# Where a chunk's first two passes over its adjacency stand in the VectorE queue of a four-layer graph network

## The chip, the cores and the metric

The kernel runs on one core of one Trainium2 chip. A core has a matrix engine (TensorE, in the profile PE, with its weight loads as PEld), a vector engine (VectorE, DVE), a scalar engine (ScalarE, ACT), a general engine (GpSimd, POOL) and a synchronisation engine (SyncE, SP), which here issues most DMA transfers. The engines run at the same time, each working through its own queue of instructions, and wait for one another through semaphores. The metric is the device time of one execution in microseconds (us), the median of several runs. The span is the same thing as one profiled execution shows it, from its first to its last instruction.

## The reference

Four layers work on a batch of 128 graphs of 64 nodes with 256 features each, and on one 64x64 adjacency matrix per graph. Each layer ends with a residual sum and a layer norm.

```python
def reference(x, adj, nodemask, ...):        # x (128, 64, 256), adj (128, 64, 64)
    # layer 0: five groups of nodes out of the first 25, two normalised graph convolutions each
    x = _layernorm(x + _L0_gnn_ref(x, adj, W1, b1, W2, b2, fusion_w))
    # layer 1: one normalised graph convolution
    x = _layernorm(x + _L1_gnn_ref(x, adj, W, b))
    # layer 2: polynomial of degree 3 in the row-normalised adjacency
    x = _layernorm(x + _L2_gnn_ref(x, adj, W, conv_w, conv_b))
    # layer 3: five steps of message passing with a GRU cell
    x = _layernorm(x + _L3_gnn_ref(x, adj, nodemask, weight, w_ih, w_hh, b_ih, b_hh))
    return x

# layer 0, for each group of nodes (25, 9, 7, 6 and 6 of them)
A = adj_g + eye;  dinv = sum(A, -1) ** -0.5
norm_adj = dinv[:, :, None] * A * dinv[:, None, :]
h   = relu(norm_adj @ (x_g @ W1[g]) + b1[g])
out = relu(norm_adj @ (h @ W2[g]) + b2[g])

# layers 1 and 2 on the whole 64x64 adjacency
deg_inv_sqrt = (adj + eye).sum(-1) ** -0.5
adj_norm = adj / (adj.sum(2, keepdims=True) + 1e-9)
```

What matters below: layer 0 makes a scaled and transposed adjacency for every group, and layers 1 to 3 make others (row sums, a normalised matrix, a matrix of zeros and ones) from the whole 64x64 adjacency of each graph.

## The kernel before

Layer 0 is cut into 16 *units*: numbers 0 to 8 belong to the four small groups of nodes, numbers 9 to 15 to the group of 25 (`g0` is 9). Layers 1 to 3 are cut into 16 *chunks* of 8 graphs. The order of TensorE's instructions is that of the program text. The other engines' instructions are put in order at compile time: an instruction may be placed ahead of others that stand before it in the text, as soon as what it needs is, by the compiler's reckoning, at hand.

A unit of layer 0 is prepared like this. It reads its slice `a` of the adjacency, takes the power -0.5 of the degrees on GpSimd, spreads the result into block-diagonal form (`A0`), has TensorE transpose it, and scales the transposes on the way out of PSUM:

```python
powers, evictions, relus = [], [], []

def prep(i):                                             # cut
    u = UNITS[i]
    scale, last = [], evictions[-1] if evictions else None
    for ts, nb, r, k in u.same:
        with tc.issue_after(last.ins) if last else nullcontext():
            nc.vector.tensor_add(ae[...], a[...], eye0[...])             # A + eye
        nc.vector.tensor_reduce(deg[:r], av, AX.X, ALU.add)
        dinv = inv_sqrt(deg[:r], w, r, "d0")             # d0z, d0s on DVE, d0r on POOL, d0o on DVE
        nc.vector.tensor_mul(av, av, dinv[...])
        nc.vector.tensor_mul(A0[...], ae[...], block0[...])              # block diagonal
        nc.tensor.transpose(p[:r, t, :r], A0[:r, t, :r], ident[:r, :r])  # one per tile
        scale.append((AT[...], p[...], dinv[...]))
    for v in scale:
        with tc.high_priority():
            evictions.append(nc.vector.tensor_mul(*v))   # the scaling of the unit's transposes
```

`tc.issue_after(ins)` makes each instruction of its block stand behind `ins` in the queue of `ins`'s engine. It adds an order at compile time and no semaphore.

A chunk of layers 1 and 2 goes through the generator `mid`; only its first piece matters here:

```python
def load_adj(c):
    a64 = keep.tile([128, NP, N], F32, name="a64", bufs=2)
    nc.sync.dma_start(a64, av[c])
    adjs[c] = a64

def mid(c):
    a64 = adjs.pop(c)
    Ab = keep.tile([128, NP, 128], F32, name="Ab", bufs=1)
    nc.vector.tensor_mul(Ab..., a64..., pair...)                    # two graphs as one 128x128 block
    A01 = keep.tile([128, NP, 128], F32, name="A01", bufs=4)
    nc.vector.tensor_scalar(A01, Ab, 0.0, None, op0=ALU.not_equal)
    rsum = small.tile([128, NP], F32, name="rsum")
    nc.vector.tensor_reduce(rsum, a64, AX.X, ALU.add)
    # rdeg, rinv, reciprocal, dinv1 = inv_sqrt(rdeg, ..., "d1"), rsum + 1e-9: small, from rsum
    nc.vector.tensor_mul(dg, ident..., rsum...)
    nc.scalar.activation(poly, dg, AF.Identity, scale=cw[:, 2:3])
    nc.vector.tensor_mul(An, Ab, rinv...)
    yield
    # ... TensorE transposes Ab (pT1), DVE makes AT1 from it
    yield
    # ... six further pieces: polynomial, gathers, products, norms
```

Layer 0's loop over the units calls pieces of the first two chunks in between (`early_stage` takes `mid(0)` and then `mid(1)` on by one `yield`):

```python
early = both(mid(0), mid(1))
places = [(1, 1), (1, 2), (2, 1), (2, 2), (2, 2), (3, 1), (3, 2), (3, 2)]
places += [(4, 0), (4, 0), (4, 1), (4, 2), (4, 2), (5, 1), (5, 2), (5, 2)]     # (i - g0, place)

for i in range(-2, NU + 1):                              # cut
    stage(load0, i + 3)
    stage(add, i - 1)
    stage(aggregate, i + 1)
    early_stage(i, 0)
    stage(support, i)
    stage(finish, i - 1, g0)
    early_stage(i, 1)
    stage(prep, i + 2)
    stage(hidden, i + 1)
    early_stage(i, 2)
    # store_others(i - 1), others(i), load_others(i + 2): layer norm of the nodes outside every group
    if i == g0:
        for c in (0, 1):
            load_adj(c)
    # ...
```

So in the program's text the first piece of `mid(0)` comes in turn i = 10, after `prep(11)` and before `prep(12)`, and that of `mid(1)` in turn i = 13, after `prep(14)`. For the chunks 2 to 15 the two loads and `mid` are called from layer 3's loop, when layer 0 has long been written down.

Of the kernel before, what the change touches and what calls it, by code (L numbers as in the profile page):

```python
# [11 lines left out]
ALU = mybir.AluOpType  # L12
AX = mybir.AxisListType
PSUM = bass.MemoryType.PSUM

B, N, D, HID, L = 128, 64, 256, 512, 5
# [11 lines left out]
NP = CB // 2  # L28
# [40 lines left out]
def gnn_stack(  # L69
# [26 lines left out]
    nc = tc.nc  # L96
# [17 lines left out]
    powers, evictions, relus = [], [], []  # L114
# [63 lines left out]
    def psum(name):  # L178
        return pt.tile([128, 512], F32, tag="pt", name=name)

    def psum0(name):

        taken[0] += 1
        if taken[0] % 8 < 5:
            return pg.tile([128, 512], F32, tag="pg", name=name)
        return psum(name)
# [33 lines left out]
    def mid(c):  # L220

        a64 = adjs.pop(c)


        Ab = keep.tile([128, NP, 128], F32, name="Ab", bufs=1)
        nc.vector.tensor_mul(
            Ab.rearrange("p q (b m) -> p q b m", b=2),
            a64[:, :, None, :].to_broadcast([128, NP, 2, N]),
            pair[:, None, :, :].to_broadcast([128, NP, 2, N]),
        )  # L230
        A01 = keep.tile([128, NP, 128], F32, name="A01", bufs=4)
        nc.vector.tensor_scalar(A01, Ab, 0.0, None, op0=ALU.not_equal)
        rsum = small.tile([128, NP], F32, name="rsum")
        nc.vector.tensor_reduce(rsum, a64, AX.X, ALU.add)
        rdeg = small.tile([128, NP], F32, name="rdeg")
        nc.vector.tensor_scalar(rdeg, rsum, 1.0, None, op0=ALU.add)
        rinv = small.tile([128, NP], F32, name="rinv")
# [17 lines left out]
        p = psum("pT1").rearrange("p (q n) -> p q n", q=NP)  # L255
# [10 lines left out]
        p = psum("pp").rearrange("p (q n) -> p q n", q=NP)  # L266
# [7 lines left out]
        p = psum("pp").rearrange("p (q n) -> p q n", q=NP)  # L274
# [6 lines left out]
        for u in range(NP // 2):  # L281
            p = psum("pd").rearrange("p (q d) -> p q d", q=2)
            for h in range(2):
                q = 2 * u + h
# [4 lines left out]
            for h in range(2):  # L289
                q = 2 * u + h  # L290
# [11 lines left out]
        for u in range(NP // 2):  # L302
            p = psum("pd").rearrange("p (q d) -> p q d", q=2)
            for h in range(2):
                q = 2 * u + h
# [5 lines left out]
            for h in range(2):  # L311
                q = 2 * u + h
# [13 lines left out]
    def const_later(src, shape, name):  # L326
        return const(src, shape, name, nc.gpsimd)
# [5 lines left out]
    with ExitStack() as c0:  # L333
# [198 lines left out]
        p = psum0("pw")  # L532
# [22 lines left out]
        def products(l, q):  # L555
# [7 lines left out]
            return p  # L563

        early = both(mid(0), mid(1))

        places = [(1, 1), (1, 2), (2, 1), (2, 2), (2, 2), (3, 1), (3, 2), (3, 2)]
# [11 lines left out]
        for i in range(-2, NU + 1):  # L579
# [54 lines left out]
            elif i == 1:  # L634
                with tc.issue_after(powers[-1].ins):
                    pair = const_later(c_pair, [128, 2, N], "pair")
# [284 lines left out]
    for s in range(NCH * L):  # L921
        u, t = s // (2 * L) * 2, s % (2 * L)
        if t == 0:
            for _ in filler:
                pass
            if u + 2 < NCH:
                for c in (u + 2, u + 3):
                    load_adj(c)
                    load_x(c)
                filler = both(mid(u + 2), mid(u + 3))  # L930
# [116 lines left out]
```

## Time and profile before

| quantity | value |
|---|---|
| device time, median of 3 runs | 2215.43 us (2214.81 to 2216.5) |
| span of the profiled execution | 2214.5 us |
| mean clock granted to TensorE | 0.994 |
| instructions | 30166 |
| HBM traffic over the span | 22 GB/s |
| DVE, two stretches of 20 us: 80 to 100 and 100 to 120 us | 5.20 and 0.75 us busy |
| ACT, the same two | 6.29 and 0.00 us busy |
| PE, the same two | 20.00 and 6.35 us busy |

Layer 0 takes roughly the first 320 us, and layers 1 to 3 the rest. An engine's busy time is the time in which an instruction of its is recorded as running. "Granted clock" is the share of full speed at which TensorE was let run. In the timelines a row gives the start in us, the time from the first to the last instruction of the row, the engine, the line of the program, the operation, the output and the inputs with their shapes, how many instructions the row merges, and in brackets how long the engine had been idle and what ended that wait. A wait is told as "engine, what it waited to do, whom it waited for".

### The profile page before, as it was taken

How to read it: one execution, taken by the hardware profiler on the slowest of the kernel's cores; microseconds unless marked ns; L12 is line 12 of the kernel's file. 1: busy time of each engine (PE TensorE's matmuls, PEld its weight loads, DVE VectorE, ACT ScalarE, POOL GpSimd, SP SyncE). 2: the span in 40 equal slices, each digit the busy share in tenths (PEclk: the TensorE clock that was granted, in tenths of full speed). 3: DMA queues.
4: the chain of work that ended last, by engine and by line, in shares of the span. 5: the costliest groups of instructions: out<-in, count | busy, mean ns of one | idle time of the engine just before them, and what ended most of it. 6: DMA issues, size and time to landing. Idle time of an engine off the chain costs nothing.

```text
span 2214.5 us, 30166 instructions
## 1 busy us (share of the span) xinstructions
PE 2180.2 (98%) x11542; PEld 1911.4 (86%) x11542; DVE 1372.5 (62%) x3088; ACT 1003.1 (45%) x1853; POOL 571.0 (26%) x621
## 2 busy tenths in 40 slices
PE   9979999999999999999999999999999999999997
PEld 6657888888889889888889898888898898888886
DVE  3344666665766666666766676657666666566546
ACT  3233334445545454445454454455454544455453
POOL 3211122222222223223222222222222232232221
PEclk9989999999999999999999999999999999999999
DMA  5531210000100000000100010001000000000000
GB/s 166 178 109 55 58 46 4 1 3 1 41 1 4 1 20 22 3 1 7 35 1 3 1 41 1 3 1 41 1 1 1 20 10 1 1 10 11 1 1 20
DMA packets 54172, 51.12 MB, mean 23 GB/s; under 512 B 20878, under 2 KB 49036, under 8 KB 54028
## 3 DMA queue, kind: packets, MB, share of 16 engines
q1 hardware_dynamic: 49664, 43.96, 6.5%
q0 software_dynamic: 1936, 4.83, 0.8%
q8 instruction: 91, 1.49, 0.3%
q10 hardware_dynamic: 2428, 0.41, 0.1%
q14 instruction: 53, 0.43, 0.1%
HBM read 32.40 MB, written 16.78 MB: 22 GB/s over the span
## 4 chain that ended last, share of the span: by engine, by line
PE 94%; SPq 2%; DVE 1%; issue 1%; DMA 1%; ACT 0%; POOL 0%; POOLq 0%; DVEq 0%; ACTq 0%
PE parz L731 25%; PE pdrz L731 12%; PE pan L731 12%; PE pa L210 9%; PE pbrz L731 6%; PE pdn L731 6%; PE pT L772 4%; PE ps L442 4%; PE ph L426 3%; PE pbn L731 3%; PE pd L286 2%; PE pd L307 2%; SPq L362 1%; PE pa L411 1%; PE po L464 1%
## 5 line engine op out<-in xcount | busy, mean ns | idle before, releaser
L748 ACT COPY c<-parz 128x512 f32<-128x512 f32 x240 | 140.6, 586 | 322.4 <-PE parz L731 321.7
L731 PE MATMUL parz<-Th,WHH 128*128 128x256 f32 x960 | 286.0, 379 | 0.3 <-ACT c L748 0.3
L731 PE MATMUL parz<-Ta,V 128*128 128x256 f32 x960 | 285.8, 379 | 0.0
L711 POOL TENSOR_TENSOR Th<-hn 128x512 f32<-128x512 f32 x64 | 81.4, 1272 | 778.3 <-DVE hn L834 602.8
L831 ACT ACTIVATE NI<-NI,bih 128x512 f32<-128x512 f32 (+1 forms) x162 | 115.9, 715 | 206.0 <-DVE NI L826 205.8
L748 ACT COPY c<-pan 128x512 f32<-128x512 f32 x237 | 139.0, 586 | 150.1 <-PE pan L731 150.1
L731 PEld LDWEIGHTS parz<-Ta,V 128*128 128x128 f32 x960 | 182.5, 190 | 24.7
L731 PEld LDWEIGHTS parz<-Th,WHH 128*128 128x128 f32 x960 | 176.5, 191 | 21.1 <-ACT c L748 0.7
L803 ACT ACTIVATE RZ<-RZ,brz 128x512 f32<-128x512 f32 x160 | 116.0, 726 | 138.9 <-DVE RZ L760 138.9
L711 POOL TENSOR_TENSOR Ta<-agg 128x512 f32<-128x512 f32 x80 | 102.0, 1275 | 260.0 <-ACT agg L214 260.0
L760 DVE TENSOR_TENSOR RZ<-pdrz,c 128x512 f32<-128x512 f32 x80 | 55.0, 688 | 173.2 <-PE pdrz L731 173.2
L139 POOL TENSOR_TENSOR rs<-ve,mhalf 128x4 f32<-128x4 f32 (+3 forms) x67 | 68.9, 1029 | 298.3 <-DVE ve L137 234.4
L731 PE MATMUL pan<-Ta,V 128*128 128x256 f32 x474 | 141.3, 380 | 0.0
L731 PE MATMUL pan<-Th,WHH 128*128 128x256 f32 x474 | 141.1, 379 | 0.0
L754 DVE TENSOR_TENSOR NI<-pbn,c 128x512 f32<-128x512 f32 x79 | 54.6, 692 | 127.8 <-PE pbn L731 110.2
L210 PEld LDWEIGHTS pa<-A,h 128*128 128x128 f32 x1024 | 124.4, 192 | 3.3
L210 PE MATMUL pa<-A,h 128*128 128x128 f32 x1024 | 124.6, 275 | 0.0
L750 DVE TENSOR_TENSOR NI<-pdn,c 128x512 f32<-128x512 f32 x79 | 54.5, 689 | 112.7 <-ACT c L748 112.7
L832 DVE TENSOR_TENSOR RZ<-hn,NI 128x512 f32<-128x512 f32 (+1 forms) x129 | 87.8, 680 | 49.5 <-ACT NI L831 49.5
L834 DVE TENSOR_TENSOR hn<-RZ,NI 128x512 f32<-128x512 f32 (+1 forms) x161 | 109.8, 682 | 1.8
L833 DVE TENSOR_TENSOR RZ<-RZ 128x512 f32<-128x512 f32 (+1 forms) x161 | 109.5, 680 | 1.8
L442 PE MATMUL ps<-W,hg 128*125 128x256 f32 (+5 forms) x464 | 103.6, 380 | 0.3 <-ACT v L313 0.3
(220 smaller groups left out, 5077.0 us busy)
## 6 DMA issues: line engine op xcount, KB each, us to landing
out_dram<-xt SPq DMA_DIRECT2D x32, 256.0 KB
W<-in_w_dram SPq DMA_DIRECT2D x10, 512.0 KB
xt<-xb SPq DMA_DIRECT2D x32, 156.0 KB
xo<-in_x_dram SPq DMA_DIRECT2D x9, 512.0 KB
xb<-xo SPq DMA_DIRECT2D x9, 512.0 KB
xt<-xa SPq DMA_DIRECT2D x32, 100.0 KB
xg<-in_x_dram SPq DMA_DIRECT2D x25, 125.0 KB
xa<-xg SPq DMA_DIRECT2D x25, 125.0 KB
```

The lines of the kernel that those rows point to most:

```text
L139: nc.gpsimd.tensor_tensor(rs[:r, :n], ve[:r, :n], mhalf[:r, :n], ALU.pow)
L210: nc.tensor.matmul(p[:, q * 128 : (q + 1) * 128], src[:, q, k * 128 : (k + 1) * 128], m[:, q, :], start=True, stop=True)
L442: nc.tensor.matmul(p[: u.rows[t], t - v, :], hg[:, e, u.off[t] : u.off[t] + u.rows[t]], W2[:, u.g, e, :], start=e == 0, stop=e == 3,)
L711: nc.gpsimd.tensor_sub(t[:, 0:2, :], a[:, :, H:], a[:, 0, :].rearrange("p (s n) -> p s n", s=2))
L731: nc.tensor.matmul(bank[:, g, :], w[:, q, i - 1, :], rhs, start=i in (1, 2, 5) and g == 0 and m == 0, stop=m == len(side) - 1, skip_group_ ...
L748: nc.scalar.copy(c, self.a)
L772: nc.tensor.transpose(p[:, q * 128 : (q + 1) * 128], src(q, k), ident)
L803: nc.scalar.activation(RZ[:, q, 0, :], RZ[:, q, 0, :], AF.Sigmoid, bias=b[0])
L831: nc.scalar.activation(n, n, AF.Tanh, bias=bih[:, 4 + j : 5 + j])
L832: e.tensor_sub(d, self.hT[:, j, f], n)
L833: e.tensor_mul(d, d, z)
L834: e.tensor_add(self.hn[:, j, f], d, n)
```

## The change

`mid`'s two instructions that read the freshly loaded adjacency of a chunk, the spreading into blocks (`Ab`) and the row sums (`rsum`), are put behind the last scaling of layer 0's transposes that the program has written down by then (`evictions[-1]`): behind unit 11's for chunk 0, unit 14's for chunk 1, and unit 15's for all later chunks. No instruction is added, removed or made cheaper, and no semaphore is set; only the order in DVE's queue is bound. The aim is that these two do not stand early in that queue and hold up instructions of layer 0 behind them.

```diff
@@ -223,15 +223,17 @@
         Ab = keep.tile([128, NP, 128], F32, name="Ab", bufs=1)
-        nc.vector.tensor_mul(
-            Ab.rearrange("p q (b m) -> p q b m", b=2),
-            a64[:, :, None, :].to_broadcast([128, NP, 2, N]),
-            pair[:, None, :, :].to_broadcast([128, NP, 2, N]),
-        )
+        with tc.issue_after(evictions[-1].ins):
+            nc.vector.tensor_mul(
+                Ab.rearrange("p q (b m) -> p q b m", b=2),
+                a64[:, :, None, :].to_broadcast([128, NP, 2, N]),
+                pair[:, None, :, :].to_broadcast([128, NP, 2, N]),
+            )
         A01 = keep.tile([128, NP, 128], F32, name="A01", bufs=4)
         nc.vector.tensor_scalar(A01, Ab, 0.0, None, op0=ALU.not_equal)
         rsum = small.tile([128, NP], F32, name="rsum")
-        nc.vector.tensor_reduce(rsum, a64, AX.X, ALU.add)
+        with tc.issue_after(evictions[-1].ins):
+            nc.vector.tensor_reduce(rsum, a64, AX.X, ALU.add)
```

## The prediction, made before the changed kernel was seen

> **What bounds the kernel now.** I read the page first: the busy line and the chain of work that ended last.
>
> ```profile
> PE 2180.2 (98%) x11542; PEld 1911.4 (86%) x11542; DVE 1372.5 (62%) x3088; ACT 1003.1 (45%) x1853; POOL 571.0 (26%) x621
> ...
> PE 94%; SPq 2%; DVE 1%; issue 1%; DMA 1%; ACT 0%; POOL 0%; POOLq 0%; DVEq 0%; ACTq 0%
> ```
>
> TensorE is busy in 2180.2 of 2214.5 us, so its idle time is 34.3 us in all. A change that only reorders DVE can win no more than that, plus what a lower clock costs. Where is the idle time? In the page's 40 slices none is empty, so I asked for busy times in stretches of layer 0. From 100 to 120 us PE is busy for 6.35 us of 20. The waits between 50 and 130 us, longest first, name the reason:
>
> ```profile
> ACT poly L248 <- DVE dg L244: 26.0, 1, 26.0
> ...
> DVE Ab L226 <- DMA a<-in_adj_dram: 25.5, 1, 25.5
> ...
> PE pT L397 <- DVE A L389: 15.1, 1, 15.1
> ...
> PE ph L426 <- ACT ag L416: 2.5, 1, 2.5
> ```
>
> (What it waited for, us in total, times, longest.) DVE stood once for 25.5 us at `Ab`, until the adjacency of a chunk landed. TensorE stood for 15.1 us at the transposes of a unit, for its block-diagonal `A0`. DVE's timeline shows that these are one event:
>
> ```profile
> 93.63 0.16 DVE L121 TENSOR_TENSOR d0s<-deg,d0z 126x4 f32<-126x4 f32 x1
> 119.25 0.69 DVE L226 TENSOR_TENSOR Ab<-a,pair 128x512 f32<-128x512 f32 x1 [25.46 <-DMA a<-in_adj_dram]
> 119.86 0.15 DVE L125 SCALAR_TENSOR_TENSOR d0o<-deg,d0r 126x4 f32<-126x4 f32 x1
> ...
> 120.68 0.75 DVE L389 TENSOR_TENSOR A<-ae,block 126x252 f32<-126x252 f32 x2
> ```
>
> `d0o` needed only GpSimd's power, which ran from 93.93 to 94.94 us. It ran at 119.86 because `Ab` of chunk 0 stood ahead of it. Counting rows back from the group of 25 (shape 125, unit 9 first), this is unit 7, prepared in turn i = 5, while `Ab` belongs to turn 10: the compiler had moved it five turns forward. Its data were not there because SP's queue came to that load late:
>
> ```profile
> 104.39 7.57 SPq L362 DMA_DIRECT2D xg<-in_x_dram  x8
> 112.00 2.35 SPq L191 DMA_DIRECT2D a<-in_adj_dram  x2
> ```
>
> TensorE's timeline gives the bill. The second part, from another stretch, is the same pair of steps (transposes of four tiles, then 16 products of 264 columns) without a disturbance:
>
> ```profile
> 99.18 7.17 PE L442 MATMUL ps<-W,hg 128*126 128x256 f32 x32
> 121.48 1.10 PE L397 MATMUL pT<-ident,A 126*126 126x126 f32 x4 [15.13 <-DVE A L389]
> 125.07 5.31 PE L426 MATMUL ph<-ag,W 128*128 128x264 f32 x16 [2.48 <-ACT ag L416]
> 130.22 1.95 PE L464 MATMUL po<-AT,s 126*128 126x126 f32 x16
> ...
> 157.24 0.60 PE L397 MATMUL pT<-ident,A 125*125 125x125 f32 x4
> 157.67 3.73 PE L426 MATMUL ph<-ag,W 128*128 128x264 f32 x16
> 161.24 1.95 PE L464 MATMUL po<-AT,s 126*128 126x126 f32 x16
> ```
>
> And the clock, in finer stretches (the number after the busy times is the granted clock):
>
> ```profile
> 105.00:110.00 5.00, 1.35 (x7) 0.84 (x5) 0.00 (x0) 0.00 (x0) 0.00 (x0) 1.00 0.58 175
> ...
> 125.00:127.50 2.50, 2.43 (x6) 1.92 (x7) 1.57 (x8) 1.53 (x5) 1.42 (x1) 0.50 0.41 152
> 127.50:130.00 2.50, 2.50 (x12) 2.11 (x11) 1.38 (x8) 1.17 (x3) 1.01 (x1) 0.88 0.32 111
> ```
>
> The stall costs twice: idle time, and half the clock until about 128 us.
>
> [...] `d0o` had its operand 25 us before it ran. [...] here eight `xg` issues took 7.57 us of SP's queue, nearly 1 us each, and the load of `a64` stood behind them[...].
>
> **The change part by part.** Nothing is removed or added. `Ab` and `rsum` of chunk 0 go behind unit 11's scaling, which ran at 188.68 us in the trace before; those of chunk 1 behind unit 14's (253.43), those of later chunks behind unit 15's (280.85).
>
> 1. What goes away. From the end of the support products (99.18 + 7.17 = 106.35 us) to the next `po` (130.22) the trace has 23.87 us. Its parts: 15.13 us idle; from the transposes to `ph` 125.07 - 121.48 = 3.59 us against 157.67 - 157.24 = 0.43 undisturbed, 3.16 too many; `ph` 130.22 - 125.07 = 5.15 us against 161.24 - 157.67 = 3.57, 1.58 too many. The sum is 15.13 + 3.16 + 1.58 = 19.87 us, all on the path, since TensorE is full before and after. For TensorE not to wait, unit 7's `A0` must be there at 106.35. With `Ab` gone `d0o` runs at about 95.0, and from it `A0`'s last row ends 120.68 + 0.75 - 119.86 = 1.6 us later at most, at 96.6: ten us early. ACT's `ag` copies also stood behind a `poly` that waited for chunk 0's `dg` (the 26.0 us above); `poly` moves with it, and the copies follow `pa`, which ended at 99.26.
>
> 2. What is moved. Chunk 0's first piece costs DVE, by start-to-start distances in the trace from 119 to 124 us, about 0.61 (`Ab`) + 0.33 (`rsum`) + 0.33 (`A01`) + 0.61 (`An`) + 0.60 (`dg`) + some 0.6 for seven small ones, 3.1 us. It now falls after unit 11's scaling, ahead of unit 12's preparation. There `A0` of unit 12 was done at 199.04 and its transposes ran at 206.54: 7.5 us of room. `Ab`'s own transposes stand at 213.69, 25 us after the new place. Chunk 1's piece, about the same, goes after 253.43; its transposes stand at 266.96, and DVE sat idle there for 3.89 us before 262.92. It fits, with less to spare, because its chain also has a GpSimd power of about 1.4 us. I put 0.5 us on the path for both. Chunks 2 and on lose only a head start that nothing used: their first piece is needed in layer 3's loop after 349 us.
>
> Sum: -19.87 + 0.5 = -19.4 us, 2215.43 - 19.4 = 2196.0 us, ratio 1.009.
>
> **The rivals.** (a) *The loads become the bound.* SP went on issuing during the stall and gained up to 20 us of lead, which TensorE would now eat up. Against it: unit 10's adjacency slice, issued from 114.44 to 119.08, is wanted at 159.99, or 140 after the change; allowing it the 7.2 us that `a64` took from issue to use leaves some 14 us. Unit 8's features, issued by 96.5, are wanted at 148.3, now 128. Unit 11's slice waits for the buffer that unit 8's reading frees, which comes forward too. If a load were late by 5 to 10 us the gain would halve: 2200 to 2206. (b) *DVE becomes the bound from 170 to 280 us*, because up to 6 us are put where 50 to 65% is busy already. The rooms of 7.5 and 3.9 us speak against it; if both failed, some 3 us each: about 2202. (c) *Another instruction takes `Ab`'s place at the head of the queue.* Only `Ab` and `rsum` read the load, and both are held, so a hold of one alone would have left the wait and the time at 2215. `A01`, `dg` and `An` need one of them. (d) *The compiler's order shifts elsewhere*, in SP's queue above all: chunk 2's load needs chunk 0's buffer, free some 50 us later than before, and a load placed too early would block those behind it. By the text's order it should follow unit 14's slice (its buffer comes free earlier), so I expect no harm; if not, 2200 or so.
>
> **Range and chances.** The 19.87 us are read directly and hardly depend on a model. The span of repeated runs is 1.7 us. Above the centre stand rivals (a), (b) and (d), below it only that my 0.5 us is not needed and that runs scatter. I take 2192 to 2201. The whole gain is 0.9%, and the largest conceivable one, all 34.3 us idle plus 3 of clock, is 1.7%, so the band of 2% should hold it: 0.98 within, 0.01 on each side.
>
> **What would show it right or wrong.** Right: no wait of DVE for the adjacency load in the profile after; unit 7's transposes directly behind the support products at about 106 us; the granted clock at 1.00 from 100 to 140 us; `po` at about 110.4 instead of 130.22; everything after it up to the end earlier by the same 19 to 20 us; chunk 0's `Ab` at about 169 to 175 us and chunk 1's at about 234 to 240. Wrong: a new idle stretch of PE before the transposes of unit 12 or of `Ab`, an SP wait for a chunk's buffer ahead of a unit's slice, or a shift at 110 us that shrinks before 330 us.

## The result, and the profile after

| | before | after |
|---|---|---|
| device time, median | 2215.97 us (4 runs, 2214.81 to 2217.66) | 2196.9 us (4 runs, 2196.56 to 2198.38) |
| ratio after to before, 95% interval | | 0.9915 (0.9897 to 0.9932) |
| span of the profiled execution | 2214.5 us | 2196.5 us |
| mean granted clock | 0.994 | 0.997 |

The change saves 0.85% of the time (0.7 to 1.0% by the interval). The forecast was 2196.0 us. The page of the changed kernel, busy line and chain of work that ended last:

```profile
PE 2178.7 (99%) x11542; PEld 1909.1 (87%) x11542; DVE 1372.8 (62%) x3088; ACT 1003.2 (46%) x1853; POOL 571.3 (26%) x621
...
PE 96%; DVE 2%; issue 1%; POOL 1%; DMA 0%; ACT 0%; ACTq 0%; POOLq 0%; DVEq 0%
```

DVE, ACT and POOL do what they did before, to within 0.3 us. The compiled program has 30178 instructions instead of 30166: the two traces differ by twelve semaphore instructions (six on DVE, four on PE, two on SP), so the binding of the order did add some, though no work. Run 8 has 30171 and gains as much, so the gain does not hang on them. The idle time of TensorE fell from 34.3 to 17.8 us, and SP's queue, 2% of the chain before, is gone from it. DVE's timeline (line numbers past `mid`'s start are up by one to two, from the two added lines) shows unit 7 prepared without a break, and the first read of chunk 0's adjacency 79 us later:

```profile
96.12 0.16 DVE L121 TENSOR_TENSOR d0s<-deg,d0z 126x4 f32<-126x4 f32 x1
97.47 0.16 DVE L125 SCALAR_TENSOR_TENSOR d0o<-deg,d0r 126x4 f32<-126x4 f32 x1 [1.18 <-POOL d0r L123]
...
97.88 0.75 DVE L391 TENSOR_TENSOR A<-ae,block 126x252 f32<-126x252 f32 x2
...
176.62 0.66 DVE L227 TENSOR_TENSOR Ab<-a,pair 128x512 f32<-128x512 f32 x1
```

The only wait left in `d0o` is the 1.18 us for GpSimd's power. The load itself came hardly earlier, as SP's timeline shows: it is issued at 110.38 us instead of 112.00, still behind eight `xg` transfers and well after `d0o`:

```profile
102.44 7.90 SPq L364 DMA_DIRECT2D xg<-in_x_dram  x8
110.38 2.31 SPq L191 DMA_DIRECT2D a<-in_adj_dram  x2
```

TensorE's timeline of the changed kernel, same four rows as before the change:

```profile
101.67 7.17 PE L444 MATMUL ps<-W,hg 128*126 128x256 f32 x32
108.68 0.60 PE L399 MATMUL pT<-ident,A 126*126 126x126 f32 x4
109.11 3.73 PE L428 MATMUL ph<-ag,W 128*128 128x264 f32 x16
112.68 1.95 PE L466 MATMUL po<-AT,s 126*128 126x126 f32 x16
```

No idle time stands in brackets any more. From the end of the support products (101.67 + 7.17 = 108.84 us) to `po` are 3.84 us instead of 23.87: 20.03 us saved. The clock (the number after the five busy times) is 1.00 in every stretch of the changed kernel from 100 to 280 us; two of them:

```profile
110.00:115.00 5.00, 5.00 (x34) 4.60 (x33) 3.81 (x22) 3.03 (x6) 1.42 (x2) 1.00 0.50 151
115.00:120.00 5.00, 5.00 (x30) 4.17 (x29) 2.63 (x13) 1.63 (x4) 0.82 (x2) 1.00 0.47 149
```

One thing looks wrong: TensorE reached the support products at 101.67 us, 2.5 us *later* than before. Run 1 takes this up.

### The profile page after: what moved, and what is told of

Read it like the earlier page. It is cut to its first block, busy times and chain, and to the rows that moved or that the text cites. A ratio compares the mean times of both kernels' runs of the same rounds, so it can differ in the third digit from the quotient of the medians.

```text
span 2196.5 us, 30178 instructions
## 1 busy us (share of the span) xinstructions
PE 2178.7 (99%) x11542; PEld 1909.1 (87%) x11542; DVE 1372.8 (62%) x3088; ACT 1003.2 (46%) x1853; POOL 571.3 (26%) x621
## 4 chain that ended last, share of the span: by engine, by line
PE 96%; DVE 2%; issue 1%; POOL 1%; DMA 0%; ACT 0%; ACTq 0%; POOLq 0%; DVEq 0%
PE parz L733 25%; PE pdrz L733 12%; PE pan L733 12%; PE pa L210 9%; PE pbrz L733 6%; PE pdn L733 6%; PE ps L444 4%; PE ph L428 4%; PE pT L774 4%; PE pbn L733 3%; PE pd L288 3%; PE pd L309 2%; PE pa L413 1%; PE po L466 1%; PE pp L278 1%
```

## The experiments

Medians in us, with the kernel before run on the same chip beside each. The ratio is not the quotient of the two medians; the two differ most where the runs of a kernel fall into groups (run 2).

| run | kernel | median | before beside it | ratio, 95% interval |
|---|---|---|---|---|
| 1 | changed kernel again | 2196.67 | 2214.14 | 0.9915 (0.9901 to 0.9930) |
| 2 | only `Ab` held | 2221.14 | 2214.14 | 1.0019 (1.0009 to 1.0028) |
| 3 | chunks 0 and 1 loaded early and bound to their old place, later chunks free | 2211.94 | 2214.14 | 0.9987 (0.9978 to 0.9996) |
| 4 | before, stall filled with products | 2213.38 | 2214.14 | 0.9994 (0.9986 to 1.0003) |
| 5 | changed, same products added | 2214.55 | 2214.19 | 0.9997 (0.9988 to 1.0005) |
| 6 | only chunk 0 held | 2197.15 | 2214.19 | 0.9919 (0.9902 to 0.9935) |
| 7 | changed, `Ab` of chunk 0 thirteen times | 2199.39 | 2214.19 | 0.9932 (0.9917 to 0.9946) |
| 8 | holds nearer to the load | 2196.39 | 2214.19 | 0.9916 (0.9901 to 0.9930) |
| 9 | as 3, later chunks held too | 2197.37 | 2214.51 | 0.9914 (0.9900 to 0.9929) |
| 10 | before again | 2217.89 (one run) | 2214.51 | |

**1. The changed kernel again.** No edit.

> The changed kernel itself once more, for a tighter interval and a second profile. In the first profile of it TensorE reached the support products of unit 6 at 101.67 us instead of 99.18, because the identity matrix landed late at the start. Theory (one wait removed, worth 19.87 us plus or minus 0.3): median about 19 to 20 us below the kernel before; from the end of those products to the next po about 3.8 us instead of 23.87. If the late start belongs to the change, the products start at 101.7 us again; if it is scatter of that one run, they start near 99.2.

The support products start at 99.59 us, so the late start was scatter. In the first profile TensorE's first transposes waited 0.92 us for the identity matrix and started at 9.48 us instead of 8.99. That is 0.5 us of the 2.08; nearly all of the rest is two steps right behind, which took 1.56 us longer while the granted clock was 0.83 and then 0.50 (10 to 12.5 and 12.5 to 15 us; before the change it was 1.00 in both, and the two steps took 8.74 us instead of 10.30). From the end of the products (106.76) to `po` (110.59) are 3.83 us, 20.04 less than before. The span is 2194.4 us, 20.1 below the first profile of before. The first profile's later start (101.67 - 99.59 = 2.08 us) is the whole difference of the two spans of this kernel (2.1 us).

**2. Only `Ab` held.**

```diff
-        with tc.issue_after(evictions[-1].ins):
-            nc.vector.tensor_reduce(rsum, a64, AX.X, ALU.add)
+        nc.vector.tensor_reduce(rsum, a64, AX.X, ALU.add)
```

> Only the spreading into blocks (Ab) is held, the row sums (rsum) are free. In DVE's queue rsum of chunk 0 then stands exactly where Ab stood, ahead of unit 7's d0o. Theory (whatever reads the load first at that place waits for it): DVE waits some 25 us in rsum, TensorE some 15 us before unit 7's transposes, time as before, 2215 to 2217 us. Rival (it is Ab's own work or the heavier pass that costs): most of the gain stays, about 2197 us.

The wait stayed, taken over by the light pass. DVE's timeline of this run:

```profile
93.60 0.15 DVE L121 TENSOR_TENSOR d0s<-deg,d0z 126x4 f32<-126x4 f32 x1
119.49 0.42 DVE L235 TENSOR_REDUCE rsum<-a 128x4 f32<-128x256 f32 x1 [25.73 <-DMA a<-in_adj_dram]
119.83 0.15 DVE L125 SCALAR_TENSOR_TENSOR d0o<-deg,d0r 126x4 f32<-126x4 f32 x1
```

It is even slower than before, by 0.2%, which I had not expected. Its twelve runs fall into two groups, five from 2216.6 to 2217.6 us and seven from 2220.9 to 2222.4; the profile is of the second. ACT's timeline, then TensorE's:

```profile
94.06 0.68 ACT L431 ACTIVATE hg<-ph,b 128x504 f32<-128x504 f32 x1 [1.01 <-PE ph L427]
122.22 0.72 ACT L249 ACTIVATE poly<-dg,cw 128x512 f32<-128x512 f32 x1 [27.48 <-DVE dg L245]
122.85 0.66 ACT L431 ACTIVATE hg<-ph,b 128x504 f32<-128x504 f32 x1
```

```profile
99.15 1.56 PE L443 MATMUL ps<-W,hg 128*126 128x256 f32 x6
123.56 8.07 PE L443 MATMUL ps<-W,hg 128*126 128x256 f32 x26 [22.86 <-ACT hg L431]
```

With `rsum` first, `dg` and the `poly` made from it were put one place further forward in ACT's queue, ahead of the last `hg`. TensorE therefore stopped inside the support products, at 100.71 us, instead of after them: 22.86 us idle instead of 15.13 + 2.48. Here one late load stopped DVE, ACT and TensorE, each at the first instruction that needed something made from it. Why the runs fall into two groups stays open.

**3. Loaded early, at the old place.** The loads of chunks 0 and 1 go from GpSimd's queue; `Ab` and `rsum` of these chunks are bound to the place that they had before the change (`lastev[6]` is unit 6's scaling).

```diff
-        nc.sync.dma_start(a64, av[c])
+        (nc.sync if c > 1 else nc.gpsimd).dma_start(a64, av[c])
 ...
+        with tc.issue_after(lastev[6].ins) if c < 2 else nullcontext():    # Ab; the same for rsum
 ...  # load_adj(0), load_adj(1) in turn i = 1 instead of i = g0
```

> The place in DVE's queue stays as before the change (Ab and rsum of chunks 0 and 1 directly in unit 7's preparation, behind unit 6's scaling), but the two adjacency loads are issued from GpSimd's queue at about 45 to 60 us instead of SP's at 112. Theory (only the wait for the load cost anything, not the place): no wait of DVE for the load, unit 7's transposes at about 106 us, time 2195 to 2198 us. Rival (the place itself holds up unit 7 because its passes stand ahead of A0): about 3 us of DVE work ahead of A0, which was due ten us before TensorE wanted it, so also little; if the place mattered, a TensorE wait of several us before unit 7's transposes would stay, 2200 us or more.

The forecast of this run failed: 2211.94 us. `Ab` no longer waited (it ran at 92.20 us), and unit 7's transposes came on time, but DVE waited again, 16.64 us, now for chunk **2**. DVE's timeline, then TensorE's:

```profile
119.76 0.42 DVE L236 TENSOR_REDUCE rsum<-a 128x4 f32<-128x256 f32 x1 [16.64 <-DMA a<-in_adj_dram]
...
122.62 0.68 DVE L403 TENSOR_TENSOR AT<-pT,d0o 126x504 f32<-126x504 f32 x1
```

```profile
111.42 1.95 PE L467 MATMUL po<-AT,s 126*128 126x126 f32 x16
123.35 3.78 PE L414 MATMUL pa<-AT,xg 126*128 126x126 f32 x16 [9.98 <-DMA xg<-in_x_dram]
```

Chunk 2's row sums, free here, had moved up behind them, ahead of unit 7's scaling (`AT`); TensorE's next step, `pa`, needs that `AT`. The profile puts TensorE's 9.98 us down to the features `xg`, but `AT` ended at 123.30 and `pa` began at 123.35. Run 9 decides between the two.

**9. The same, with the later chunks held.**

```diff
-        with tc.issue_after(lastev[6].ins) if c < 2 else nullcontext():    # both passes
+        with tc.issue_after(lastev[6 if c < 2 else NU - 1].ins):
```

> The third experiment left a wait of 16.6 us: with chunks 0 and 1 loaded early, chunk 2's free row sums stood ahead of unit 7's scaling and waited for chunk 2's load, which needs chunk 0's buffer and SP's queue. Here chunks 0 and 1 are loaded early and stay at their old place in unit 7's preparation, and the two passes of chunk 2 and later are held behind unit 15's scaling. Theory (any reader of a load not yet landed at the head of DVE's queue costs, and nothing else; the old place is harmless once its data are there): no wait of DVE for an adjacency load, no TensorE wait around 106 to 125 us, 2195 to 2198 us. Rival (the old place ahead of unit 7's A0 costs by itself, or TensorE's 10 us wait in the third experiment was for the features xg that the profile names): a wait of some us stays, 2200 to 2208 us.

2197.37 us, the gain of the change. DVE's timeline, then TensorE's:

```profile
91.80 0.67 DVE L227 TENSOR_TENSOR Ab<-a,pair 128x512 f32<-128x512 f32 x1
95.25 0.41 DVE L236 TENSOR_REDUCE rsum<-a 128x4 f32<-128x256 f32 x1
...
97.39 0.72 DVE L391 TENSOR_TENSOR A<-ae,block 126x252 f32<-126x252 f32 x2
```

```profile
100.01 7.17 PE L445 MATMUL ps<-W,hg 128*126 128x256 f32 x32
107.02 0.60 PE L399 MATMUL pT<-ident,A 126*126 126x126 f32 x4
...
112.80 1.95 PE L414 MATMUL pa<-AT,xg 126*128 126x126 f32 x16
```

`Ab` and the row sums stand ahead of unit 7's `A0`, as before the change, and cost nothing, because their data are there. `pa` starts at 112.80 without a wait, although SP issued the `xg` loads of this stretch later than in run 3 (from 92.38 us against 87.42, the next ones from 105.34 against 103.05): the wait in run 3 was for `AT`. So the place was harmless and the missing data were the cause, which runs 2, 3 and 9 show together.

**4 and 5. The stall filled.** Nothing uses the added products; they only occupy TensorE.

```diff
+                if i == 7:
+                    pw = psum("pfill")
+                    for _ in range(19):
+                        nc.tensor.matmul(pw, ident, W1[:, 1, 0, :], start=True, stop=True)
                 for t in range(ts.start, ts.stop):
                     nc.tensor.transpose(p[:r, t, :r], A0[:r, t, :r], ident[:r, :r])
```

> The kernel before, with 19 products of 512 columns into a spare bank put into TensorE's queue just ahead of unit 7's transposes; nothing uses them. At full clock each takes about 0.89 us, 16.9 us in all, so they fill the stall of 15.13 us and a little more. Theory (idle time 17.6 us, half clock 2.3 us): the clock stays at 1.00, the transposes and ph run at full speed, ph still starts when the ag copies are there at about 125 us, po at about 128.6 instead of 130.2: 1.5 us faster than the kernel before, about 2214 us. Rival (added work adds to a busy engine): 2215.5 + 17 = 2232 us.

> The changed kernel with the same 19 unused products of 512 columns ahead of unit 7's transposes. Theory (TensorE is full there after the change, so the stretch counts one to one): 16.9 us are added, about 2196.9 + 16.9 = 2213.8 us, within 1.5 us of the kernel before with the same filling: once the stall is filled with other work the change is worth next to nothing. Rival (another wait behind takes part of them in): clearly less is added, 2205 us or so.

TensorE in run 4, the kernel before with the products, and the clock in one of its stretches:

```profile
107.15 16.47 PE L400 MATMUL pfill<-W,ident 128*128 128x512 f32 x38
123.46 0.59 PE L402 MATMUL pT<-ident,A 126*126 126x126 f32 x4
124.14 3.83 PE L431 MATMUL ph<-ag,W 128*128 128x264 f32 x16
127.81 1.95 PE L469 MATMUL po<-AT,s 126*128 126x126 f32 x16
```

```profile
115.00:120.00 5.00, 5.00 (x13) 2.15 (x12) 1.68 (x6) 0.00 (x0) 0.00 (x0) 1.00 0.44 135
```

The products take 123.46 - 107.15 = 16.31 us, 0.86 each (the 0.89 expected was an estimate; 16 support products of 256 columns in 7.17 us make 0.90 for 512), and cost the kernel before nothing that its time shows (interval from -0.14% to +0.03%): they run in the stall. With TensorE busy there the clock was 1.00 in every stretch from 100 to 130 us (in the first profile of before 0.60 from 110 to 115 us, 0.50 from 115 to 127.5 and 0.88 from 127.5 to 130), the transposes took 0.59 us instead of 1.10, and `ph` 3.67 instead of 5.15. So this slow part of the stall's bill came from TensorE standing still. From the transposes to `ph` are 0.68 us instead of 3.59; most of that difference is the wait for ACT's `ag` (2.48 us before), which the products now cover for the most part, and not the clock. The 1.5 us by which this run should have been faster can't be told from nothing. Added to the changed kernel the same products cost their full length. TensorE in run 5:

```profile
100.03 7.17 PE L449 MATMUL ps<-W,hg 128*126 128x256 f32 x32
...
127.34 1.95 PE L471 MATMUL po<-AT,s 126*128 126x126 f32 x16
```

The span is 2211.2 us, 16.8 above run 1, and from the start of the support products to `po` TensorE takes 27.31 us (100.03 to 127.34), against 27.67 in run 4 (100.14 to 127.81). With the hole filled the change is worth 0.4 us in the traces, and by the medians of the two runs (2213.38 and 2214.55 us, on two chips) nothing. What it takes away is time in which TensorE stood still, with the lower clock (0.50) that was recorded in it and just behind it.

**6. Only chunk 0 held.** Both holds get `if c == 0 else nullcontext()`.

> Only chunk 0's two passes are held; chunk 1's and the later ones are free, and the compiler puts them where they were before the change (Ab of chunk 1 behind AT1 of chunk 0). Theory (only chunk 0's hold carries the gain): as the changed kernel, 2196 to 2198 us, and the 0.27 us that TensorE waited at the transposes of chunk 1's Ab goes away. Rival (the free row sums of chunks 1 and 2 wait for their loads at the head of the queue instead): a new wait of DVE for an adjacency load, and a time between 2198 and 2216 us.

2197.15 us: chunk 0's hold carries the gain, and the free row sums of chunks 1 and 2 wait for no load, since with chunk 0 late they come late by themselves. The 0.27 us before the transposes of chunk 1's `Ab` are gone (1.79 us from `pa` to these transposes instead of 2.06), too little for the time to show.

**7. The room on DVE behind unit 11.** Chunk 0's `tensor_mul` for `Ab` inside the hold is repeated 13 times.

> The changed kernel with chunk 0's Ab computed 13 times instead of once, all behind unit 11's scaling, to measure the room that DVE has there. 12 more passes of about 0.61 us are 7.3 us. In the profile of the changed kernel A0 of unit 12 is done at 185.97 us and its transposes run at 189.00, 3.0 us later, and DVE idles for 0.7 + 0.9 + 0.9 us in between, which the passes can use. Theory (room of 3.0 us plus up to 2.5 us of idle time): TensorE waits 1.8 to 4.3 us before unit 12's transposes, time 2199 to 2201 us. Rival (DVE is half idle there, it takes them in): no wait, 2197 us. Rival (no room at all): 2204 us.

TensorE in this run:

```profile
186.24 1.04 PE L502 MATMUL pse<-ident,z 128*125 128x128 f32 x8
189.13 0.67 PE L400 MATMUL pT<-ident,A 125*125 125x125 f32 x4 [1.86 <-DVE A L392]
```

TensorE waited 1.86 us, and the time rose by 2.7 us over run 1 (spans: 2.4). So of 7.3 us added 5.4 did not reach TensorE. The 3.0 us of slack ahead of unit 12's transposes took their part. The other 2.4 us did not even delay `A0`: DVE's timeline shows that the compiler put two passes of the piece, `A01` and `An` (0.94 us), behind `A0`, so the estimated 1.5 us that is left fell into DVE's waits for GpSimd. The limit that the prediction counted on is real, and the change stays within it.

**8. Holds nearer to the load.** Chunk 0 behind unit 8's scaling, chunk 1 behind unit 11's, later ones behind unit 15's:

```diff
-        with tc.issue_after(evictions[-1].ins):
+        with tc.issue_after(lastev[{0: 8, 1: 11}.get(c, NU - 1)].ins):    # Ab; the same for rsum
```

> The changed kernel with the holds nearer to the load: chunk 0 behind unit 8's scaling (about 122 us, when its adjacency landed some 5 us earlier) and chunk 1 behind unit 11's, where the compiler puts Ab of chunk 1 behind AT1 of chunk 0; later chunks as in the changed kernel. Theory: the whole gain needs no more than a place behind the landing; no wait for the load, unit 12's A0 is done 3 to 4 us earlier, the 0.27 us before the transposes of chunk 1's Ab go away, so 2196.5 us, not to be told from the changed kernel by its time. Rival (the later place matters): a wait of DVE for the load at about 122 us and some us lost.

2196.39 us, not to be told from the change's 2196.67 (run 1). `Ab` ran at 122.71 us without a wait; unit 12's `A0` was done at 181.08 us and wanted at 187.33, so 6.2 us of room are left instead of 3.0. It is the safer place, and no faster one.

**10. The kernel before once more.** No edit.

> The kernel before once more, for a second profile: its times on these chips scatter from 2212 to 2220 us, while those of the changed kernel lie within 1 us. If the scatter comes from when the load lands, DVE's wait at Ab and TensorE's wait before unit 7's transposes differ from the 25.5 and 15.1 us of the first profile by about as much as the two spans differ.

TensorE's timeline of this second profile of before:

```profile
104.17 7.17 PE L442 MATMUL ps<-W,hg 128*126 128x256 f32 x32
122.27 1.10 PE L397 MATMUL pT<-ident,A 126*126 126x126 f32 x4 [10.93 <-DVE A L389]
125.86 6.55 PE L426 MATMUL ph<-ag,W 128*128 128x264 f32 x16 [2.49 <-ACT ag L416]
132.25 1.95 PE L464 MATMUL po<-AT,s 126*128 126x126 f32 x16
```

Here TensorE came to the stall 5.0 us later than in the first profile (104.17 against 99.18), after a wait of 2.89 us at the start and products behind it (`ph`) that took 8.72 us instead of 7.02, while SP issued the load at 112.94 instead of 112.00. DVE waited 21.26 us for it and TensorE idled for 10.93 us instead of 15.13, both 4.2 us less, while the span is 1.6 us longer: the forecast of this run failed. `po` came only 2.0 us later, 0.8 of them because `Ab` ran later (120.03 against 119.25), and 1.2 because `ph` took 6.39 us instead of 5.15. In this profile the clock was 0.50 from 115 to 130 us and still below 1.00 after that (the last three numbers of a row are the clock, the DMA share and GB/s):

```profile
130.00:132.50 2.50, 2.50 (x11) 2.06 (x10) 2.39 (x13) 0.80 (x3) 0.07 (x1) 0.72 0.11 39
```

In the first profile the clock is 0.88 already from 127.5 to 130 us, and 1.00 after that; what sets the length of the slow stretch is not shown. So in these two profiles the load, and not TensorE's arrival, set when the stall ended. It does not explain why the kernel before scatters over 8 us in 31 runs: a stall with such an end evens out a late start (here 5.0 us of it), and run 5, which has no such wait, scatters over 3 us in 12 runs. The three of the 31 runs above 2219 us have a mean granted clock of 0.993, the fastest one 0.995, so more time at the lower clock goes with the long runs; whether it is their cause stays open.

## Why the prediction was right, step by step

**What goes away (19.87 us).** Measured 20.03 and 20.04 us in two profiles of the change against the first profile of before. All three parts went: the idle time (15.13 us), the wait for the late `ag` copies (2.48 us), the half clock (0.50 from 115 to 127.5 us before, 1.00 after). The size belongs to that one execution, though. In the second profile of before (run 10) 20.91 us lie between the end of the support products and `po`, so there only 17.1 us would go away, because TensorE came later and stood idle for less. The claim that unit 7's `A0` would be ready ten us early held: its last row ended at 98.63 us, TensorE wanted it at 108.68.

**What is moved (0.5 us on the path).** Unit 12's transposes did not wait. But the 3.1 us of the piece took 4.4 us of the 7.5 us of room: `A0` of unit 12 ended at 185.97 us and was wanted at 189.00. DVE's timeline after the change:

```profile
182.47 0.16 DVE L125 SCALAR_TENSOR_TENSOR d1o<-rdeg,d1r 128x4 f32<-128x4 f32 x1 [0.90 <-POOL d1r L123]
...
184.80 0.16 DVE L125 SCALAR_TENSOR_TENSOR d0o<-deg,d0r 125x4 f32<-125x4 f32 x1 [0.90 <-POOL d0r L123]
...
185.29 0.68 DVE L391 TENSOR_TENSOR A<-ae,block 125x500 f32<-125x500 f32 x1
```

The terms left out are the first wait, 0.90 us for the piece's own power on GpSimd, in which DVE stood, and 0.48 us because unit 12's power took 1.48 us instead of 1.01 (from `d0s` to `d0o` 1.76 us instead of 1.28). The second wait is no new one: it was 1.12 us before. Chunk 1 cost 0.27 us, in both profiles of the change. TensorE's timeline:

```profile
247.63 1.95 PE L413 MATMUL pa<-AT,xg 125*128 125x125 f32 x16
249.69 0.66 PE L259 MATMUL pT<-ident,Ab 128*128 128x128 f32 x4
```

From one to the next are 2.06 us, and 1.79 in the kernel before. So 0.27 instead of 0.5.

**The sum.** Predicted 19.4 us and 2196.0; measured a span 20.1 us shorter when both start nearly alike (run 1 against the first profile of before), and medians 19.1 us apart, 2196.9. Of the 20.1 us, 19.6 are there by the products `pa` at 327.01 us of before (307.45 in run 1); the other 0.5 arose behind it, and why is not shown. The 0.9 us between forecast and median are less than the spread of the four runs (1.8 us). But against 31 runs of before the gain is 17.5 us (2214.14 to 2196.67), and 17.0 and 17.8 us for the variants of runs 6 and 8: less than the 19.4 forecast. The base of 2215.43 us and the bill of 19.87 came from the same three runs of a kernel whose stall varies, so the forecast of the time held better than that of the gain; that it fell within 0.9 us is in part luck. The mechanism is no luck: runs 2, 3 and 9 show it.

**The rivals.** (a) No load became the bound: TensorE's waits after the change hold none for a unit's loads. (b) DVE did not become the bound; run 7 shows that with 7.3 us more at chunk 0's place TensorE would have waited for it, though only 1.86 us. (c) It did not happen, and run 2 shows that it would have with one of the two passes free, though at 2221 us and not at 2215, because ACT's queue was caught earlier; run 3 shows it with chunk 2. (d) The order in SP's queue did shift, chunk 2's load going out at 177.70 us instead of 120.37, behind unit 14's slice and ahead of unit 15's (180.12). SP waited 0.7 us for chunk 0's buffer there, which is one of the signs of being wrong that the prediction names; it held up no work of TensorE.

**The marks.** `po` at 112.68 us instead of the 110.4 named, 110.59 in run 1; chunk 0's `Ab` at 176.62, just past the 169 to 175 named, 174.53 in run 1; chunk 1's at 236.63, inside 234 to 240.

## What to carry to other kernels

When an engine's long wait for a load ends and its neighbours' waits end with it, look at what stood behind the waiting instruction: in the kernel before one early read of late data kept `d0o`, whose operand was there at 94.94 us, in DVE's queue until 119.86, and ACT stood for 26.0 us and TensorE for 15.13, each at the first instruction that needed something made behind that read. Either have the data there or put the read behind work that does not need it; hold every instruction that reads the load (run 2), and look where the later rounds' readers then stand: free ones moved up and waited in run 3, and waited for nothing in run 6. Weigh the new place by the time at which the next product is wanted, and count in the waits that the moved chain brings along.

## What the runs showed that I had not expected

An early disturbance is passed on differently by the two kernels: TensorE came 5.0 us late in the kernel before and was 2.0 us late at `po` (run 10 against the first profile), and even these came from a later load (0.8 us) and from a clock that was 0.50 up to 130 us instead of 127.5 (1.2 us), as the stall took in all of the late start; in the changed kernel 2.08 us of late start are 2.1 us of span. These are one pair of profiles each. And the engine that the profile names as the one waited for can be the wrong one of two: in run 3 it named a load, and what ended the wait was a DVE pass 0.05 us earlier.
